# Near scans with B's product on GpSimd, the mean of D u and of near sums taken off early, and a hand-ordered tail

## The chip, the core and the metric

The kernel runs on one core of a Trainium2 chip. Five engines work side by side, each through its own list of instructions in order: TensorE (PE, matmuls into PSUM), VectorE (DVE), ScalarE (ACT), GpSimd (POOL) and SyncE (SP, which here only issues DMAs). They wait for each other through semaphores. The metric is the device time of one execution in microseconds, the median of several runs.

## What is computed

Two layers over a 64 x 64 image with 96 channels. Each layer normalises, projects to 192 inner channels, convolves 3 x 3, and runs four selective scans over the 4096 positions; their sum is normalised over the channels, gated and projected back, and added to the input. The change lies in the first layer, whose scan and end are:

```python
dt = softplus(dt @ dt_proj_w + dt_proj_b)
log_dA = einsum('bld,dn->bldn', dt, A)
dB_u = einsum('bld,bln->bldn', dt, B_mat) * u[..., None]
decay = exp(cumsum(log_dA, axis=1))
h = decay * cumsum(dB_u / (decay + 1e-12), axis=1)
y = einsum('bldn,bln->bld', h, C_mat) + u * D_skip
...
y = y1 + y2 + back(y3) + back(y4)          # rows, rows backwards, columns, columns backwards
y = _layernorm(y, ln_g, ln_b)              # over the 192 channels
y = y * silu(z)
return y @ out_proj_w
```

`decay` falls below 1e-12 after a short stretch, so that far from a scan's start `h` is almost nothing. The kernel uses this: it computes the scans of the first layer only near their starts, finds out whether that covers them, and only otherwise runs the far scans.

## The kernel before

The inner channels and positions are folded into three blocks T of 128 partitions: `u[T]` (the convolved input) and `y[T]` (the sums) are 128 x 2048. A chunk c is 512 of the 2048 columns; there are four, worked from 3 down to 0.

Work of the first layer in this order: `head` (norm, projection, convolution, gate), `near_scans` (lines 277 to 612), the branch (`tc.If`, line 1729) with `far_scans` in it, `tail` (lines 1471 to 1546). Then the second layer's head, its 384 scan steps of 128 x 1024, and its end. In the input timed the branch is not taken: the far scans do not run.

**Near part.** For each block T the first 192 steps of the four directions are laid side by side (768 columns). Buffers in order: `nu` (u gathered by TensorE), `nus` (its copy), `npj` and `nxd` (the projections to B, C and dt), `npd` (dt), then softplus in `nw`, `nln`, `nt`, `nv`; `ndt`, `ndu = dt * u` and `nS` (the running sum of dt) are each copied to the other half of the partitions by SP's DMAs (`across`). Of the 16 states, taken in pairs m, the first pair is kept for 192 steps, the second for 64, the other six for 32 (`kinds`). That gives six units j: block T with 768 columns (the first pair) or with 256 + 768 (the rest), in the order 0a, 0b, 1a, 1b, 2b, 2a. For each unit:

- `operands`: `nna = exp(-A dt)` on ScalarE, with GpSimd clearing the first column of each part
- `weights_of`: `nnwt`, a tanh of S, on ScalarE
- `scan`: VectorE multiplies B by du into `nb` (PSUM), multiplies by 1 + `nnwt`, scans into `nnh`; GpSimd (VectorE in the last unit) makes `nnhc = nnh * C`
- `add`: TensorE sums the pairs into `ny` (PSUM), and after both units of a block `sum_up` adds `ny` to `y[T]` on VectorE

B comes from TensorE: a 0/1 matrix `picked` spreads each row of B over 64 partitions, into the four PSUM banks `nB`. C goes to DRAM (`nC`) and comes back spread over the partitions (`ncb`). `y` itself begins as u times D: `later`, six passes on GpSimd (`start_y`) at the beginning. `reach` and `reached` work out the flag of the branch. `look_ahead` issues the second layer's weights on SP; `ds` of the second layer is reduced on VectorE when its part of them has landed.

**Tail.** For each chunk: `centre` (mean of y over the channels by TensorE with the matrix `pos`, taken off by VectorE, then squared on ScalarE), `scale` (variance by TensorE, then rstd by Ln and Exp on ScalarE), `gated` (two operations on VectorE for each block), `project` (TensorE, then the add to the residual, the statistics for the next norm, and the store).

What sets the order: instructions issued through `pe`, `act`, `dve`, `pool` and `sp` keep the order in which they are written; those issued through `nc.vector` and so on, as in this tail, are placed by the framework's scheduler. ScalarE's function tables are loaded by the kernel (`load_exp_ln` loads the one that has Exp and Ln both) and, where a function might be called without its table, by the framework, which adds a load ahead of it.

Most instructions of the near part carry the line of the recording helper, 271, in the profile; tile names tell them apart.

Of the kernel before, what the change touches and what calls it, by code (L numbers as in the profile page):

```python
# [9 lines left out]
F32 = mybir.dt.float32  # L10
BF16 = mybir.dt.bfloat16
AF = mybir.ActivationFunctionType
ALU = mybir.AluOpType
# [31 lines left out]
def two_ss2d_layers(  # L45
# [231 lines left out]
    def near_scans(weights, later):  # L277
# [5 lines left out]
        with ExitStack() as sc:  # L283
# [5 lines left out]
            def parts(t):  # L289
# [9 lines left out]
            kinds = ((NEAR, 0, 1),) + FEWER  # L299
            top = once.tile([128, len(kinds), 3, 4], F32, name="top")  # L300
            most = once.tile([128, len(kinds) + 1, 3], F32, name="most")
            flag = once.tile([1, 1], mybir.dt.int32, name="flag")
            picked = once.tile([32, NP, 128], F32, name="picked")
            nc.gpsimd.tensor_copy(
                picked.rearrange("p m (h w) -> p m h w", h=2),
                i3[0:32, 0:NS].rearrange("p (m h) -> p m h", h=2)
                .unsqueeze(3)
                .to_broadcast([32, NP, 2, 64]),
            )
            for start in later:  # L310
                start()


            us = once.tile([128, 3, 2, 2 * NEAR], F32, name="nus")
            k = NEAR // HW
            pj = pps.tile([128, 2, 512], F32, tag="m", name="npj")[0:NC, :, 0 : 2 * NEAR]
            for T in range(3):
                ps = pps.tile(
                    [128, 4 if T == 2 else 2, 512], F32, tag="yBB"[T], name=f"nu{T}"
                )[:, 0:2]  # L320
# [18 lines left out]
                for q, copy in enumerate((act.copy, dve.tensor_copy)):  # L339
                    copy(us[:, T, q], ps[:, q, 0 : 2 * NEAR])  # L340
            for T in range(3):
                for q in range(2):
                    pe.matmul(
                        pj[:, q], xw[HALF[q], 0, T, :], us[HALF[q], T, q],
                        start=(T == 0), stop=(T == 2),
                    )
# [6 lines left out]
            C = []  # L353
            for w, m0, m1 in kinds:
                rows = dram.tile([NS, 4 * w], F32, name=f"nC{w}")
                sp.dma_start(
                    out=rows.rearrange("n (d w) -> n d w", w=w),
                    in_=parts(xd[NC - NS : NC])[:, :, 0:w],
                )
                C.append(rows)  # L360


# [62 lines left out]
            def reach():  # L425
# [10 lines left out]
                pe.transpose(Bf[0:1, at : at + 128], most[:, len(kinds), 0:1], ident)  # L436

            def reached():
                ps = Bf[0:1, at : at + 128]
                dve.reduce_max(most[0:1, len(kinds), 1:2], ps, axis=AX.X)  # L440
                dve.tensor_scalar(flag, most[0:1, len(kinds), 1:2], GONE, None, ALU.is_le)


            Bp = pps.tile([128, 4, 512], F32, tag="B", name="nB")
            Bf = Bp.rearrange("p a b -> p (a b)")
            B, cb, at = [], [], 0
            for n, m0, m1 in kinds:
                B.append([])
                t = once.tile([128, m1 - m0, 4 * n], F32, name=f"ncb{n}")
                for m in range(m0, m1):  # L450
                    dst = Bf[:, at : at + 4 * n]
                    if n == NEAR:
                        for s in (slice(0, 512), slice(512, WN)):
                            pe.matmul(
                                dst[:, s], picked[:, m, :], xd[0:32, s], start=True, stop=True
                            )
                    else:
                        pe.matmul(
                            dst.rearrange("p (d w) -> p d w", w=n), picked[:, m, :],
                            parts(xd[0:32])[:, :, 0:n], start=True, stop=True,  # L460
                        )
                    at += 4 * n
                for h, half in enumerate(HALF):
                    rows = C[len(cb)][2 * m0 + h : 2 * m1 : 2]
                    sp.dma_start(out=t[half], in_=rows.unsqueeze(0).to_broadcast(t[half].shape))
                B[-1] = Bf[:, at - 4 * n * (m1 - m0) : at]
                cb.append(t.rearrange("p n w -> p (n w)"))
# [4 lines left out]
            live = {}  # L472
# [40 lines left out]
            def scan(j):  # L513
                T, ks = units[j]
                a, wt, h, hc = live[j]

                b = pps.tile([128, 2, 512], F32, tag="m", name=f"nb{j}")
                b = b.rearrange("p a w -> p (a w)")
                o = 0
                for i in ks:  # L520
                    n, m0, m1 = kinds[i]
                    k = m1 - m0
                    dve.tensor_mul(
# [5 lines left out]
                b = b[:, 0:o]  # L529
                dve.scalar_tensor_tensor(b, wt, 1.0, b, ALU.add, ALU.mult)  # L530
# [50 lines left out]

            steps_of(0)
            steps_of(1)
            sums_of(0)
            steps_of(2)
# [6 lines left out]
            look_ahead()  # L592
            for j in range(len(units)):
# [4 lines left out]
                scan(j)  # L598
                if j == 1:
                    reach()  # L600
                if j == 2:
                    reached()
                if j == 4:
                    sum_up(1)
                add(j)
                if j == 3:
                    sum_up(0)
            sum_up(2)
            return nc.values_load(
# [860 lines left out]

    def tail(l, w, xT):
# [3 lines left out]
        with ExitStack() as sc:  # L1475
# [3 lines left out]
            sz = {}  # L1479
            for c in order:  # L1480
                for T in range(3):
# [3 lines left out]
                    nc.sync.dma_start(out=t, in_=szd[l][T, :, HT * c : HT * (c + 1)])  # L1485
                cut = slice(TC * c, TC * (c + 1))
                nc.sync.dma_start(out=xT[:, cut], in_=xs[:, cut])
            live = {}

            def centre(c):  # L1490
                cut = slice(HT * c, HT * (c + 1))
                pm = fps.tile([128, HT], F32, tag="m", name=f"m_{l}_{c}")
                for T in range(3):
                    nc.tensor.matmul(pm, pos, y[T][:, cut], start=(T == 0), stop=(T == 2))
                for T in range(3):
                    nc.vector.tensor_sub(y[T][:, cut], y[T][:, cut], pm)
                    sq = live[c, T] = fin.tile([128, HT], F32, tag=f"sq{T}", name=f"sq{l}_{c}_{T}")
                    nc.scalar.activation(sq, y[T][:, cut], AF.Square)

            def scale(c):  # L1500
                cut = slice(HT * c, HT * (c + 1))
                pv = fps.tile([128, HT], F32, tag="v", name=f"v_{l}_{c}", bufs=1)
                for T in range(3):
                    nc.tensor.matmul(pv, pos, live[c, T], start=(T == 0), stop=(T == 2))
                rstd = live[c] = fin.tile([128, HT], F32, tag="rstd", name=f"rstd{l}_{c}")
                if c == order[0]:
                    load_exp_ln()
                nc.scalar.activation(rstd, pv, AF.Ln, bias=eps5)
                nc.scalar.activation(rstd, rstd, AF.Exp, scale=-0.5)

            def gated(c):
                cut = slice(HT * c, HT * (c + 1))
                rstd = live.pop(c)
                for T in range(3):
                    q = live[c, T] = fin.tile([128, HT], F32, tag=f"g{T}", name=f"g{l}_{c}_{T}")
                    gain, bias = v[:, T, V_G : V_G + 1], v[:, T, V_B : V_B + 1]
# [304 lines left out]
```

## Time and profile before

| | us |
|---|---|
| median of 3 runs | 1474.97 |
| lowest, highest | 1471.23, 1476.99 |
| the profiled execution | 1471.02 |
| its span, first to last instruction | 1469.2 |
| near part, from the first nu matmul | 74.0 to 146.7 |
| the branch, nothing runs | 146.7 to 149.4 |
| tail of the first layer, to the last statistics | 149.4 to 192.8 |

A row of the timeline gives start, duration, engine, line, operation, the tile written and those read, and in brackets how long the engine stood idle before it and what ended the wait. A row of groups gives the count, busy microseconds, mean nanoseconds of one, and the idle time before them. A row of stages gives each engine's busy time in a stretch, TensorE's granted clock and the DMA engines' busy share. SPq is SP's queue of DMA issues. A span is the slowest core's; here there is only one.

### The profile page before, as it was taken

The numbers are of one execution on the slowest core, as the hardware profiler recorded it, in microseconds if no ns is written. First come the engines' busy times: TensorE is split into PE (matmuls) and PEld (weight loads), VectorE is DVE, ScalarE is ACT, GpSimd is POOL, SyncE is SP. The second block draws the span as 40 slices with busy tenths as digits, with TensorE's granted clock in tenths as the row PEclk, the third lists the DMA queues.
The fourth block names the chain that finished last, engine by engine and source line by source line (L and its number), as shares of the span: only waits on it lengthen the run. The fifth ranks groups of instructions, "written<-read, shape, count | busy, mean of one in ns | idle before, by whom it ended". The sixth has DMA issues, their size and how long they took to land.

```text
span 1469.2 us, 17235 instructions
## 1 busy us (share of the span) xinstructions
PE 1205.7 (82%) x5011; PEld 469.7 (32%) x5011; DVE 1338.4 (91%) x925; ACT 1216.5 (83%) x2506; POOL 1211.8 (82%) x667
## 2 busy tenths in 40 slices
PE   5845869788888797978888888887888888887887
PEld 2233313333333332333333333333333333322333
DVE  5967677789999999999999999999999999999996
ACT  5764437699998989999999999899898989897874
POOL 2753039688989898989898989898989898989894
PEclk7965979599999999999999999999999899999999
DMA  3231522526262626262626262626262726262533
GB/s 108 76 100 24 149 52 90 131 58 145 58 145 58 145 59 144 60 144 60 144 59 144 60 143 60 144 59 143 60 148 61 151 61 144 69 147 68 136 107 108
DMA packets 85556, 147.70 MB, mean 101 GB/s; under 512 B 33436, under 2 KB 36700, under 8 KB 85356
## 3 DMA queue, kind: packets, MB, share of 16 engines
q1 hardware_dynamic: 83772, 143.96, 41.3%
q0 software_dynamic: 576, 1.57, 0.5%
q10 hardware_dynamic: 1104, 0.98, 0.2%
q8 instruction: 41, 0.67, 0.2%
q14 instruction: 63, 0.52, 0.1%
HBM read 80.85 MB, written 12.13 MB: 63 GB/s over the span
## 4 chain that ended last, share of the span: by engine, by line
DVE 28%; issue 22%; PE 11%; POOL 11%; ACT 9%; DMA 6%; SPq 2%; DVEq 0%; POOLq 0%; ACTq 0%
DVE h L751 18%; DVE b L751 8%; POOL hc L751 7%; DMA cb<-C 4%; ACT a L751 3%; PE ys L751 3%; ACT bT L751 2%; SPq L751 2%; PE pj L751 2%; POOL sp L751 2%; PE b L751 1%; POOL ln L751 1%; DMA xT<-xs 1%; PE cp L271 1%; DMA dt<-sp 1%
## 5 line engine op out<-in xcount | busy, mean ns | idle before, releaser
L751 POOL TENSOR_TENSOR hc<-h,cb 128x1024 f32<-128x1024 f32 x384 | 901.9, 2368 | 93.6 <-DMA cb<-C 35.6
L751 DVE TENSOR_TENSOR_SCAN h<-a,carry,b 128x1024 f32<-128x1024 f32 x288 | 665.0, 2338 | 23.4 <-POOL hc L751 1.7
L751 ACT ACTIVATE a<-dt,am 128x1024 f32<-128x1024 f32 x384 | 438.0, 1141 | 57.3 <-DVE h L751 53.8
L751 PE MATMUL ys<-hc,fold 128*64 128x512 f32 x1536 | 429.3, 638 | 0.1
L751 ACT ACTIVATE bT<-duT,BT 128x192 f32<-128x192 f32 x1012 | 386.6, 445 | 2.9 <-PE b L751 0.9
L751 PE MATMUL b<-ident,bT 128*128 128x128 f32 x1536 | 224.3, 289 | 31.0 <-DVE h L751 19.3
L751 DVE TENSOR_TENSOR b<-b,du 128x1024 f32<-128x1024 f32 x192 | 232.0, 1208 | 6.8 <-PE b L751 6.8
L751 DVE TENSOR_TENSOR_SCAN h<-a,b 128x1024 f32<-128x1024 f32 x96 | 216.4, 2278 | 13.7 <-PE b L751 5.3
L751 PEld LDWEIGHTS b<-ident,bT 128*128 128x128 f32 x1536 | 177.0, 146 | 156.3 <-DVE h L751 89.5
L751 PE MATMUL b<-B,selh 96*128 96x512 bf16 x384 | 116.6, 385 | 126.3 <-DVE h L751 125.8
L751 PEld LDWEIGHTS ys<-hc,fold 128*64 128x64 f32 x1536 | 77.7, 138 | 138.5 <-issue 98.2
L751 PEld LDWEIGHTS <-selh 96*128 96x128 bf16 x384 | 25.6, 97 | 254.3 <-DVE h L751 203.8
L271 POOL TENSOR_TENSOR tap<-tap,tap 128x512 f32<-128x512 f32 x48 | 60.9, 1273 | 44.6 <-ACT tap L271 42.2
L751 PE MATMUL pj<-u,xw 64*124 64x512 f32 x192 | 94.1, 635 | 2.2 <-DVE w L751 1.2
L271 DVE SCALAR_TENSOR_TENSOR acc<-pad,v,acc 128x1052 f32<-128x1052 f32 (+1 forms) x64 | 75.2, 1181 | 2.1
L751 ACT CAST B<-pj 96x512 bf16<-96x512 f32 (+2 forms) x96 | 54.9, 575 | 4.5 <-PE pj L751 4.5
L751 PE MATMUL ys<-y,ident 128*128 128x512 f32 (+1 forms) x120 | 57.7, 581 | 0.0
L751 POOL TENSOR_TENSOR sp<-sp,ln 128x512 f32<-128x512 f32 x45 | 57.5, 1279 | 0.2
L751 POOL TENSOR_TENSOR ln<-ln,w 128x512 f32<-128x512 f32 x45 | 57.6, 1280 | 0.0
L751 POOL TENSOR_TENSOR su<-sp,u 128x512 f32<-128x512 f32 x45 | 57.3, 1274 | 0.0
L751 PE MATMUL pd<-xd,dwb 29*64 29x512 f32 x192 | 54.7, 639 | 0.0
L751 PEld LDWEIGHTS pj<-u,xw 64*124 64x124 f32 x192 | 33.8, 191 | 60.1 <-issue 45.7
(188 smaller groups left out, 1185.9 us busy)
## 6 DMA issues: line engine op xcount, KB each, us to landing
cb<-C SPq DMA_DIRECT2D x256, 256.0 KB
dt<-sp SPq DMA_DIRECT2D x192, 128.0 KB
du<-su SPq DMA_DIRECT2D x180, 128.0 KB
szd<-sz SPq DMA_DIRECT2D x24, 256.0 KB
szt<-szd SPq DMA_DIRECT2D x24, 256.0 KB
xT<-xs SPq DMA_DIRECT2D x8, 384.0 KB
xs<-xT SPq DMA_DIRECT2D x1, 1536.0 KB
xs<-xT SPq DMA_DIRECT2D x8, 192.0 KB
```

What stands on the lines that cost most here:

```text
L271: return lambda *args, **more: tc.keep_in_program_order(op(*args, **more))
L751: return lambda *args, **more: tc.keep_in_program_order(op(*args, **more))
```

## The change

In `near_scans`:

- B goes to DRAM and comes back spread over the partitions as C does (`stored`, `fetched`): rows of 64 steps are cut from those of 192, so that there are two stores instead of three for each of the two. The fetch of C's shorter rows is issued after block 1's transfers. `picked` and the matmuls of `nB` go.
- B's product with du is made by GpSimd (`inputs`), into SBUF tiles `nb`, the first two ahead of the units and then two units ahead; VectorE's product with the weights reads it and writes PSUM (`nbw`).
- `later` is no longer run. Instead TensorE forms the mean over the channels of D u (`mean`, with `average` = `pos` scaled by D, made by ScalarE), and VectorE writes y = D u - mean (`centre`), for chunks 3 and 2 before the units and 1 and 0 after units 0 and 1.
- The near sums change the mean of near positions again: `near_mean` forms the mean of y there (it is D u's centred value plus the near sums), `near_centre` takes it off, after the last sum. A matmul with `zeros` opens the accumulation.
- PSUM: `nu` uses three buffers instead of two; `npj` and the flag's transpose have one of their own.

In the tail: no mean and no centring; the order on each engine is written out; block 2 is gated by GpSimd with ScalarE in between (`pool_gated`), blocks 0 and 1 by VectorE; `load_exp_ln` stands at the beginning. Where the far scans run, `centre_all` takes the mean off after them.

```diff
+            for T in range(3):
+                act.mul(average[:, T], pos, ds[:, T : T + 1])
+            def mean(c):
...
+                for T in range(3):
+                    pe.matmul(
+                        ps, average[:, T], u[T][:, HT * c : HT * (c + 1)],
+                        start=(T == 0), stop=(T == 2),
+                    )
+            def centre(c):
...
+                    dve.scalar_tensor_tensor(
+                        y[T][:, s], u[T][:, s], ds[:, T : T + 1], ps, ALU.mult, ALU.subtract
+                    )
...
+            rows = stored("B", 0)
+            B = [fetched("B", rows, i) for i in range(len(kinds))]
+            rows = stored("C", NC - NS)
+            cb = [fetched("C", rows, 0)]
...
-            def scan(j):
+            def inputs(j):
...
-                    dve.tensor_mul(
+                    pool.tensor_mul(
                         b[:, o : o + 4 * n * k].rearrange("p (n d w) -> p n d w", n=k, w=n),
                         B[i].rearrange("p (n d w) -> p n d w", n=k, w=n),
                         four(du, T)[:, :, 0:n].unsqueeze(1).to_broadcast([128, k, 4, n]),
                     )
...
-                dve.scalar_tensor_tensor(b, wt, 1.0, b, ALU.add, ALU.mult)
+                dve.scalar_tensor_tensor(b, wt, 1.0, live.pop(("b", j))[:, 0:w], ALU.add, ALU.mult)
...
             steps_of(0)
+            inputs(0)
+            inputs(1)
             steps_of(1)
+            cb += [fetched("C", rows, i) for i in range(1, len(kinds))]
             sums_of(0)
+            mean(3)
+            mean(2)
...
             look_ahead()
+            for c in (3, 2):
+                centre(c)
+            for c in (1, 0):
+                mean(c)
             for j in range(len(units)):
...
                 scan(j)
+                if j < 2:
+                    centre(1 - j)
+                if j + 2 < len(units):
+                    inputs(j + 2)
...
                 if j == 4:
                     sum_up(1)
+                    near_mean(0)
+                    near_mean(1)
                 add(j)
                 if j == 3:
                     sum_up(0)
             sum_up(2)
+            near_mean(2)
+            for T in range(3):
+                near_centre(T)
```

The tail after the change, its order and the two kinds of gating:

```python
def pool_gated(c, T):
    q, gain, bias = result(c, T)
    pool.tensor_mul(q, y[T][:, at(c)], live["r", c])
    act.activation(q, q, AF.Identity, bias=bias, scale=gain)
    pool.tensor_mul(q, q, sz[c, T])
...
load_exp_ln()
squares(3)
variance(3)
squares(2)
root(3)
for c in order:
    if c:
        variance(c - 1)
    pool_gated(c, 2)
    for T in (0, 1):
        gated(c, T)
    if c > 1:
        squares(c - 2)
    if c:
        root(c - 1)
    project(c)
    if c < NCH - 1:
        add(c + 1)
add(0)
```

`squares`, `variance`, `root`, `gated`, `project` and `add` do what the steps of the same kind did before.

## The prediction

> **What bounds the kernel now.** I read the span in slices first (layer 1's scans, from 250 us on, keep VectorE at nine tenths and the diff does not touch them), then cut the part that it does touch into stages, then read each engine's timeline there. The stages:
>
> ```profile
> core 0: us, PE busy (x) PEld busy (x) DVE busy (x) ACT busy (x) POOL busy (x), PEclk, DMA share, GB/s
> 103.00:146.70 43.70, 19.36 (x57) 13.28 (x57) 32.88 (x47) 20.75 (x50) 11.79 (x16) 0.56 0.25 45
> 146.70:149.40 2.70, 0.00 (x0) 0.00 (x0) 0.00 (x0) 0.00 (x0) 0.00 (x0) 0.80 0.04 12
> 163.00:192.80 29.80, 23.61 (x72) 7.93 (x70) 29.45 (x46) 10.01 (x21) 1.52 (x13) 0.94 0.40 96
> ```
>
> The near scans are a chain through VectorE with holes (32.9 of 43.7 us busy); the branch costs 2.70 us in which nothing runs, and starts when VectorE's last near sum ends; the tail from 163 on is VectorE without a hole (29.45 of 29.80). The timeline, with what each row waited for:
>
> ```profile
> 76.42 16.95 POOL L271 TENSOR_SCALAR y<-u,ds 128x1024 f32<-128x1024 f32 x6
> 84.85 2.91 DVE L247 TENSOR_SCALAR am<-am 128x24 f32<-128x24 f32 x1
> 87.80 2.79 DVE L248 TENSOR_SCALAR am<-am 128x24 f32<-128x24 f32 x1
> 91.42 0.49 ACT L271 ACTIVATE nw<-npd 128x384 f32<-128x384 f32 x1 [2.69 <-DVE nv L271]
> 102.65 1.20 SPq L271 DMA_DIRECT2D nS<-nS  x2
> 105.52 1.03 ACT L271 ACTIVATE nnwt<-nS,lneps,am 128x768 f32<-128x768 f32 x1 [2.38 <-DMA nS<-nS]
> 144.74 1.95 DVE L271 TENSOR_TENSOR y<-ny,y 64x192 f32<-64x192 f32 x6 [3.02 <-PE ny L271]
> 160.30 1.28 ACT L85 ACT_TABLE_LOAD   x1
> 161.60 0.69 ACT L1508 ACTIVATE rstd<-v,eps 128x512 f32<-128x512 f32 x1
> 162.32 0.63 ACT L1509 ACTIVATE rstd<-rstd 128x512 f32<-128x512 f32 x1
> ```
>
> Two operations on 24 elements take 2.9 us each because GpSimd's six passes of 2.83 us run beside them; ScalarE then waits 2.69 us for VectorE. The first scan's weights wait for the transfer of S, the tenth of a queue of half-tile transfers. One table load serves the tail's Ln and Exp. Groups of the tail, by shape:
>
> ```profile
> L1520 DVE SCALAR_TENSOR_TENSOR g<-g,v,szt 128x512 f32<-128x512 f32 x12 | 8.6, 746 | 0.1
> L1517 DVE SCALAR_TENSOR_TENSOR g<-y,v,rstd 128x512 f32<-128x512 f32 x12 | 8.6, 745 | 3.5 <-ACT rstd L1509 3.4
> L1496 DVE TENSOR_TENSOR y<-y,m 128x512 f32<-128x512 f32 x12 | 7.7, 679 | 5.5 <-PE m L1494 5.5
> L1498 ACT ACTIVATE sq<-y 128x512 f32<-128x512 f32 x12 | 7.2, 627 | 34.8 <-DVE y L1496 34.7 <-DMA szt<-szd 0.2
> ```
>
> **What the Trainium skill says.** "ScalarE: Activation LUTs", What ACT_TABLE_LOAD costs: a load takes about 1283 ns and a drain about 1380 ns more. The trace agrees on the load (1.28) and shows no drain (the next operation starts 1.30 after); I use 1.30. "SBUF — State Buffer", Who interferes with whom: VectorE in a two-port mode, or with two SBUF inputs while GpSimd reads SBUF, blocks against GpSimd for whole instructions. The two am rows agree with the first half; against the second, VectorE's wl operations on two SBUF inputs took 0.69 us beside GpSimd's TENSOR_SCALAR at 256.7 and without it at 261.0. No row shows them beside a GpSimd TENSOR_TENSOR. "TensorE: Matmul & The Clock Gate", Part 1: TensorE is at half clock until it has been busy for some microseconds. Agrees: 0.50 from 88 to 132, and 0.61 and then 1.00 after the tail's matmuls begin at 149.5.
>
> **The change part by part.** *Start of the near part.* The third nu tile no longer shares a buffer with the second: the 1.16 us that PE waits at 79.37 goes. GpSimd's 16.95 us of y go too, so the am operations take some 0.2 us each: the softplus of block 1 starts at 87.7 instead of 91.4, and all that follows on ScalarE is 3.7 us earlier. The three `average` products (0.30 each, the diag row) fit in the 0.93 us in which ScalarE waits before nus.
>
> *The SP queue takes it back.* In the built program of the changed kernel 31 transfers stand ahead of the first pair of S, from the ab load at 83.6 on (before: 84.7), at 0.64 each: that pair is issued at 103.4 (before: 102.65). Ahead of it lie 384 KB of C before dt and 512 KB after du, at about 200 GB/s (the rate from 90 to 94), and eight half tiles of 96 KB at 0.65 us each: S lands 1.3 us later than before (0.8 if only the issue counts, 2.8 if C moves at the 152 GB/s of the half tiles). So the weights of unit 0 start at 106.8, those of unit 1 end at 113.8 (before: 112.6).
>
> *The units.* VectorE loses the nine products with B (6 x 0.96 + 3 x 0.43 = 7.1 us) and gains twelve centre operations of about 0.72 (8.6 us). Of these six stand before unit 0's weights are there (cover: the wait for S; without it they cost 4.3 us), three beside unit 1's tanh, three after scan 1 with no cover: 2.2 us. Unit by unit: scan 0 ends at 110.7, scan 1 at 117.5, scan 2 at 123.2 (before 121.1). GpSimd makes hc (1.81 or 2.54) and then the product two units on (the same), so product 3 is ready at 122.7, against 123.65 when VectorE asks. Scan 3 ends at 127.3 (126.4), sum 0 at 129.3. Now the missing product counts: scan 4 ends at 132.9 (133.6). TensorE's 6.3 us of ny, which wait for sum 0, end at 135.7, sum 1 at 137.7 (136.8). Ahead of the last two adds TensorE now has the zeros and two near means; at full clock, having been busy for 6 us, 0.8 + 1.3 + 1.3 us, the last behind sum 1. hc of the last unit is ready at 141.6 (141.7), the last sum ends at 146.2 (146.7).
>
> *After the last sum, uncovered:* the third near mean, eight records of 192 or 96 columns (1.3 us at full, 2.2 at half clock, taken as 1.9), and twelve small subtractions at the 0.33 of the near sums, 3.9 us, with two hand-overs 0.2: 6.0 us. The branch, and with it the tail, starts at 152.2 + 2.7 instead of 149.4: **+5.5 us**.
>
> *The tail.* Gone are twelve subtractions (7.7 us of VectorE) and four mean products. But the built program moves the tail's one load of the common Ln and Exp table ahead of the branch, where only one of the two ways is sure to pass it, and puts a load of its own before the squares, before every Ln and before every Exp: nine in the tail and two in the next head where there was one. From the tail's start: load 1.30, six squares 3.65, load, Ln, load, Exp (1.3 + 0.7 + 1.3 + 0.65): first rstd at 9.05 (before 13.6). From one rstd to the next, all in ScalarE's order: GpSimd's product 1.27 with 0.2 of hand-over, the affine 0.60, three squares 1.82, loads, Ln and Exp 3.95: 7.84 us; twice so, and once without squares, 6.02: last rstd at 30.75. VectorE needs only 5.8 us a chunk and waits. Then four g operations, 3.1, the third chunk's add and statistics 2.6, the last one's 2.6: end at 39.0, where it was 192.8 - 149.4 = 43.4: **-4.4 us**. The next head's Exp meets one more load: **+1.3 us**. Loads of szt and xT (17 us of DMA) land before they are asked for, and SP's weights end about 44 us in, before the borders at 52.
>
> *Two SBUF inputs.* The weight product in the near units has its second operand in SBUF now (it was in PSUM), and the g operations, which had both there, now run beside GpSimd's TENSOR_TENSOR. Nothing (the wl rows) to whole blocking: then units 1 to 4 wait 0.5, 0.6, 1.5 and 0.6 us, of which 2.6 stay at the last sum, and the tail's last chunk 2.6, together 5.2. I take 1.2, six weight products at the 0.19 by which one nw operation at 91.3 was longer than its fellows.
>
> Sum: 5.5 - 4.4 + 1.3 + 1.2 = +3.6 us on the profiled execution's own 1471.0 us (span 1469.2 and 1.8 around it). The median of the runs, 1474.97, lies 4.0 above it, so 1478.5. This kernel's runs spread by 0.4%, so that half a per cent, 7.4 us, is about what can be told from no change.
>
> **The rivals.** *Whole blocking between VectorE and GpSimd:* 5.2 in place of 1.2, +7.6: 1482.5. For it: the page and the am rows; against: the wl rows. *TensorE stays at half clock* after sum 0 (it decides from add 4 on): zeros 1.5, two means 2.2 each, add 4 at 4.1 and add 5 at 3.0 put the last sum at 150.6 instead of 146.2, +4.4 and 0.3 in the last mean; with the 1.2 +8.3: 1483.3, slower. For it: the clock of 0.50 through most of the stage; against: 0.71 from 132 to 140 after less work. *The loads stay hidden*, VectorE bounds the tail: rstd from 5.2 on, end at 30.2, -13.2 and no 1.3; without blocking 5.5 - 13.2 = -7.7: 1467.3. For it: 10 us of ScalarE against 30 of VectorE in the tail before; against: a load stands between each Ln and its Exp, where nothing can hide it.
>
> **How the numbers follow.** Forecast 0.56, blocking 0.18, half clock 0.14, hidden loads 0.12. The first lies within half a per cent nearly whole, 0.07 of it above; the blocking case is half above; most of the half-clock case is above: slower 0.27, faster 0.10, same 0.63. Range 1468 to 1487: from the hidden loads' time to that of half clock with S 1.5 us later and 2 us for the spread of a median.
>
> **What would show it.** Right: eleven loads of 1.28 on ScalarE in the tail and the next head, rstd 7.8 us apart, VectorE's am rows near 0.2, S landing near 106.8, and some 6 us between the last sum and the branch. Wrong: g or nbw operations of more than a microsecond (blocking), near means of 2 us (half clock), or VectorE without holes in the tail (loads hidden).

## The result and the profile after

The changed kernel takes 1484.1 us (median of 15 runs, 1478.09 to 1493.08); the kernel before, run beside it, 1471.23 (1465.64 to 1480.17). The ratio is 1.0088, with a 95% interval from 1.0067 to 1.0109: slower by 12.9 us, where 3.6 were forecast. A second set of six runs gave 1.0104 (1.0076 to 1.0131). The profiled execution took 1493.08 us, 9 above the median, at a mean granted TensorE clock of 0.922 (0.932 in the median run); a second profile of the same kernel has a span of 1483.6 at 0.927.

To compare profiles whose heads begin at slightly different times, I count from the start of the last eight z matmuls of the first head, which the change leaves alone. All entries are us from the timelines; the branch is counted up to VectorE's first instruction behind it (the memset of dwb), the tail from there to the aggregation of its statistics, the next head to the first operation on wl in layer 2, and the rest to the end of the span.

| profile | z to last near sum | mean of near tokens, and branch | tail | next head | rest of layer 2 | clock |
|---|---|---|---|---|---|---|
| before | 74.55 | 2.95 | 43.24 | 63.78 | 1212.5 | 0.930 |
| before, again | 72.31 | 2.96 | 43.42 | 63.91 | 1214.1 | 0.940 |
| after | 78.13 | 6.76 | 43.79 | 66.21 | 1222.8 | 0.922 |
| after, again | 78.11 | 7.00 | 43.39 | 66.16 | 1216.2 | 0.927 |

To the first wl operation the two kernels differ by 11.2 us (means of two), and every stage has a part in it: 4.7, 3.9, 0.3 and 2.3. The tail, which was to pay for the rest, gained nothing. Stages of the profile after: the near units up to the last sum, the mean of near tokens with the branch, and the tail behind its first rstd:

```profile
core 0: us, PE busy (x) PEld busy (x) DVE busy (x) ACT busy (x) POOL busy (x), PEclk, DMA share, GB/s
107.50:151.57 44.07, 23.28 (x85) 14.46 (x83) 35.44 (x44) 22.00 (x50) 22.06 (x22) 0.70 0.22 44
151.57:158.14 6.57, 1.16 (x8) 0.72 (x8) 3.08 (x12) 0.00 (x0) 0.00 (x0) 0.73 0.02 6
171.80:201.60 29.80, 20.99 (x56) 6.38 (x56) 24.77 (x29) 20.03 (x29) 10.05 (x20) 0.83 0.42 104
```

VectorE, which gave nine products away in the near units (7.1 us), is busier there than before (35.4 against 32.9 us). Six of the twelve centre operations stand in this stretch (4.1 us), the six products with the weights take 11.0 us instead of 6.6, and the three operations on top, which work out the flag, 1.4 instead of 0.3. In the tail ScalarE's busy time has doubled (20.0 us, where it was 10.0). First two weight products of the kernel before, then rows of the near part after:

```profile
112.66 1.23 DVE L271 SCALAR_TENSOR_TENSOR nb<-nnwt,nb 128x1024 f32<-128x1024 f32 x1
118.27 0.96 DVE L271 SCALAR_TENSOR_TENSOR nb<-nnwt,nb 128x768 f32<-128x768 f32 x1
```

```profile
85.53 0.17 DVE L247 TENSOR_SCALAR am<-am 128x24 f32<-128x24 f32 x1
85.73 0.18 DVE L248 TENSOR_SCALAR am<-am 128x24 f32<-128x24 f32 x1
...
103.22 2.61 SPq L271 DMA_DIRECT2D nCb<-nC  x4
105.94 1.21 SPq L271 DMA_DIRECT2D nS<-nS  x2
...
109.96 1.03 ACT L271 ACTIVATE nnwt<-nS,lneps,am 128x768 f32<-128x768 f32 x1 [6.25 <-DMA nS<-nS]
...
124.90 2.42 DVE L271 SCALAR_TENSOR_TENSOR nbw<-nnwt,nb 128x768 f32<-128x768 f32 x1
...
129.47 2.75 DVE L271 SCALAR_TENSOR_TENSOR nbw<-nnwt,nb 128x1024 f32<-128x1024 f32 x1
...
131.09 3.47 POOL L271 TENSOR_TENSOR nb<-nBb,ndu 128x256 f32<-128x256 f32 x2
...
136.52 1.28 ACT L85 ACT_TABLE_LOAD   x1
...
149.60 1.97 DVE L271 TENSOR_TENSOR y<-ny,y 64x192 f32<-64x192 f32 x6 [1.66 <-PE ny L271]
...
152.82 3.18 DVE L271 TENSOR_TENSOR y<-y,nmn 64x174 f32<-64x174 f32 x12 [1.25 <-PE nmn L271]
```

The am operations fell from 2.9 to 0.2 us. But S is issued later and lands later. The weight product took 0.96 us for 768 columns and 1.23 for 1024 when one of its operands lay in PSUM; now it takes 1.8 to 2.75 in four of the six units (two of them shown), each time beside a product of GpSimd's. I call this blocking. GpSimd suffers too: 3.47 us for a pair of products that took 2.51 for the unit before. The load at 136.52 is the one of Exp and Ln that the tail's code asks for: the built program runs it ahead of the branch. The tail's groups, where the kernel before had a single table load:

```profile
L271 ACT ACT_TABLE_LOAD x10 | 12.8, 1283 | 20.5 <-DVEq L1811 20.3
L271 DVE SCALAR_TENSOR_TENSOR g<-y,v,rstd 128x512 f32<-128x512 f32 x8 | 10.2, 1276 | 12.4 <-ACT rstd L271 12.4
L271 DVE SCALAR_TENSOR_TENSOR g<-g,v,szt 128x512 f32<-128x512 f32 x8 | 8.8, 1106 | 0.3
```

The g operations average 1.28 and 1.11 us where they took 0.75. Sixteen of them cost VectorE 19.0 us, and the 24 of before cost 17.2: the third that went to GpSimd bought nothing. VectorE's g operations for the third chunk and for the beginning of the last one, the last rstd, two projections, and the last wait:

```profile
183.93 1.86 DVE L271 SCALAR_TENSOR_TENSOR g<-y,v,rstd 128x512 f32<-128x512 f32 x1
185.83 0.75 DVE L271 SCALAR_TENSOR_TENSOR g<-g,v,szt 128x512 f32<-128x512 f32 x1
186.50 1.75 DVE L271 SCALAR_TENSOR_TENSOR g<-y,v,rstd 128x512 f32<-128x512 f32 x1
188.29 0.75 DVE L271 SCALAR_TENSOR_TENSOR g<-g,v,szt 128x512 f32<-128x512 f32 x1
...
189.09 1.96 PE L271 MATMUL o<-g,op 64*96 64x512 f32 x8 [1.35 <-DVE g L271]
189.41 0.63 ACT L271 ACTIVATE rstd<-rstd 128x512 f32<-128x512 f32 x1
191.60 0.73 DVE L271 SCALAR_TENSOR_TENSOR g<-y,v,rstd 128x512 f32<-128x512 f32 x1
192.36 1.81 DVE L271 SCALAR_TENSOR_TENSOR g<-g,v,szt 128x512 f32<-128x512 f32 x1
...
195.68 3.57 PE L271 MATMUL o<-g,op 64*96 64x512 f32 x8 [0.35 <-DVE g L271]
...
199.30 0.69 DVE L271 TENSOR_TENSOR xT<-o,xT 96x512 f32<-96x512 f32 x1 [1.04 <-PE o L271]
```

None of VectorE's rows of the third chunk has a wait in brackets. VectorE, slowed, no longer keeps up even with a ScalarE that is slowed by its loads: the last rstd is ready at 190.04 us, and VectorE takes it up at 191.60.

### The profile page after: what moved, and what is told of

Same layout as the page of the kernel before. It is cut to its first block, busy times and chain, and to the rows that moved or that the text cites. A ratio compares the mean times of both kernels' runs of the same rounds, so it can differ in the third digit from the quotient of the medians.

```text
span 1491.1 us, 17293 instructions
## 1 busy us (share of the span) xinstructions
PE 1225.7 (82%) x5019; PEld 471.8 (32%) x5019; DVE 1338.8 (90%) x920; ACT 1234.6 (83%) x2524; POOL 1220.4 (82%) x678
## 4 chain that ended last, share of the span: by engine, by line
DVE 23%; issue 19%; PE 14%; ACT 13%; POOL 8%; DMA 8%; SPq 5%; DVEq 0%; POOLq 0%; ACTq 0%
DVE h L805 15%; DVE b L805 6%; POOL hc L805 5%; DMA cb<-C 4%; ACT a L805 4%; PE pj L805 4%; SPq L805 3%; ACT bT L805 3%; PE ys L805 3%; PE b L805 2%; DMA dt<-sp 2%; DMA szt<-szd 1%; POOL sp L805 1%; PE cp L271 1%; POOL ln L805 1%
## 5 line engine op out<-in xcount | busy, mean ns | idle before, releaser
L805 PE MATMUL ys<-hc,fold 128*64 128x512 f32 x1536 | 434.0, 645 | 0.6 <-POOL hc L805 0.5
L805 DVE TENSOR_TENSOR b<-b,du 128x1024 f32<-128x1024 f32 x192 | 232.1, 1209 | 11.4 <-PE b L805 11.4
L805 PE MATMUL pj<-u,xw 64*124 64x512 f32 x192 | 101.4, 677 | 1.7 <-DVE w L805 1.2
L805 PE MATMUL ys<-y,ident 128*128 128x512 f32 (+1 forms) x120 | 61.0, 610 | 0.0
```

Source lines behind the costliest of these rows:

```text
L805: return lambda *args, **more: tc.keep_in_program_order(op(*args, **more))
```

## The experiments

All are edits of the changed kernel unless said otherwise. Beside each time stands its ratio to the kernel before, run with it. Theory A is the table loads, B the blocking between VectorE and GpSimd, C the mean of near tokens, D the place of S on SP's queue; what each expects stands in the text put down before the run. Times after "the z matmuls" count from their start, as in the table above.

### One table load for the tail

```diff
-            load_exp_ln()
             squares(3)
             variance(3)
             squares(2)
+            load_exp_ln()
             root(3)
```

> The changed kernel with one edit: the tail's load of the common Ln and Exp table stands behind the squares of the first two chunks instead of at the start, so that one load serves the tail, as before the change (11 loads fewer). Theory A, the loads are what the tail lost: first rstd 6.4 us after the tail's start instead of 9.8, the next ones less than 6 us apart, tail 33 us instead of 43.9, the next head 1.3 us shorter: 12 us less than the changed kernel's 1484.1, about 1472. Theory B, VectorE's g operations held up by GpSimd's products (8 of 16 took 1.63 to 1.86 us instead of 0.75) bound the tail as soon as the loads are gone: rstd early, but a chunk still takes VectorE 7.5 us or more, tail 37 to 39 us: about 1477.

Measured: 1474.48 us, ratio 1.0021 (1.0008 to 1.0034), between the two theories. The tail takes 37.24 us instead of 43.4 to 43.8, which is theory B's number: the loads cost 6.3 us there, and behind them stands VectorE. The next head takes 65.07 instead of 66.2; what the load costs there is set out below. VectorE's two groups of g operations, in this kernel's tail:

```profile
L271 DVE SCALAR_TENSOR_TENSOR g<-y,v,rstd 128x512 f32<-128x512 f32 x8 | 9.6, 1199 | 7.5 <-ACT rstd L271 7.5
L271 DVE SCALAR_TENSOR_TENSOR g<-g,v,szt 128x512 f32<-128x512 f32 x8 | 8.7, 1085 | 0.3
```

The idle time before them has fallen from 12.4 to 7.5 us, nearly all of it the wait for the first rstd; the operations are nearly as long as without this edit.

### One operand of the g operations in PSUM

This stands on top of the edit above. The variance has one PSUM buffer instead of two besides.

```diff
+                rp = live["rp", c] = fps.tile([128, HT], F32, tag="rp", name=f"rp{l}_{c}")
+                act.activation(rp, r, AF.Exp, scale=-0.5)
                 act.activation(r, r, AF.Exp, scale=-0.5)
...
+                p = fps.tile([128, HT], F32, tag="gp", name=f"gp{l}_{c}_{T}", bufs=1)
                 dve.scalar_tensor_tensor(
-                    q, y[T][:, at(c)], gain, live["r", c], ALU.mult, ALU.mult
+                    p, y[T][:, at(c)], gain, live["rp", c], ALU.mult, ALU.mult
                 )
-                dve.scalar_tensor_tensor(q, q, bias, sz[c, T], ALU.add, ALU.mult)
+                dve.scalar_tensor_tensor(q, p, bias, sz[c, T], ALU.add, ALU.mult)
```

> As e1_table, and in the tail rstd is made twice by ScalarE, once in PSUM for VectorE and once in SBUF for GpSimd, and the g operations' intermediate lies in PSUM: each of VectorE's two g operations has one operand in SBUF. Theory B (two SBUF operands beside GpSimd's products is what blocks): all 16 g operations at 0.75 us or less, GpSimd's at 1.27, tail 31 to 32 us, 5 to 7 us less than e1_table, about 1470. Theory A (only the loads counted): no difference from e1_table except 0.65 us of ScalarE a chunk, 0 to 2 us more.

Measured: 1469.78 us, 0.9996 (0.9969 to 1.0023); tail 33.41 us. The same two groups:

```profile
L271 DVE SCALAR_TENSOR_TENSOR g<-gp,v,szt 128x512 f32<-128x512 f32 x8 | 6.0, 750 | 0.4
L271 DVE SCALAR_TENSOR_TENSOR gp<-y,v,rp 128x512 f32<-128x512 f32 x8 | 6.0, 750 | 9.3 <-ACT rp L271 9.2
```

All sixteen are back at 750 ns, and the tail is 3.8 us shorter, though ScalarE makes rstd twice. What changed for VectorE is where one input of each g operation, and the first one's result, lies: theory B holds in the tail, with less than was expected of it (5 to 7 us).

### The near weights in PSUM

The buffer of the flag's transpose moves from tag j to tag B besides.

```diff
+                wt = pps.tile([128, 2, 512], F32, tag="mj"[j % 2], name=f"nwt{j}")
+                wt = live["wt", j] = wt.rearrange("p a w -> p (a w)")
...
-                b = pps.tile([128, 2, 512], F32, tag="m", name=f"nbw{j}")
-                b = b.rearrange("p a w -> p (a w)")[:, 0:w]
-                dve.scalar_tensor_tensor(b, wt, 1.0, live.pop(("b", j))[:, 0:w], ALU.add, ALU.mult)
+                b = live.pop(("wt", j))[:, 0:w]
+                dve.scalar_tensor_tensor(b, b, 1.0, live.pop(("b", j))[:, 0:w], ALU.add, ALU.mult)
```

> The changed kernel with one edit in the near part alone: the weights nnwt (tanh of S) are written to PSUM, in two buffers by turns, and VectorE's product with GpSimd's nb is made in place there, so that it has one operand in SBUF. Theory B (blocking is what the near part lost): the product takes 0.97 us in every unit instead of 2.02, 2.42, 2.75 and 1.82 in units 1 to 4, GpSimd's nb at 2.5 and 1.8, and the last near sum is 3 to 5 us earlier: about 1480. Theory C (the near part lost by S landing 2.3 us later and by the mean and the subtractions after the last sum, 4.4 us): VectorE then waits for GpSimd's products or for hc instead, the last sum less than 1.5 us earlier: about 1483.

Measured: 1487.04 us (7 runs, median clock 0.928), 1.0098 (1.0064 to 1.0131). The time shows no gain; its interval is too wide for an effect of 2 us, and I go by the trace. The products of units 2 and 3 in VectorE's timeline:

```profile
123.65 0.95 DVE L271 SCALAR_TENSOR_TENSOR nwt<-nwt,nb 128x768 f32<-128x768 f32 x1
...
126.75 1.23 DVE L271 SCALAR_TENSOR_TENSOR nwt<-nwt,nb 128x1024 f32<-128x1024 f32 x1
```

The blocking of these products is gone, 4.4 us by the sum over units 1 to 4 (9.0 and 4.6). The last sum comes 75.76 us after the z matmuls instead of 78.12, so 2.4 us of it were on the path; the rest turned into waits for the weights. After the last sum the near mean and the branch take some 0.6 us more, as TensorE's eight matmuls took 1.74 us instead of 1.16. This lies between the two theories: B in kind, half of it in size.

### All three

The three edits above in one kernel.

> The edits of e1_table, e2_tail_psum and e3_near_psum together. If loads (12 to 13 us) and blocking (tail with the loads gone 5 us, near 4 us) are the whole of what went wrong: near part 2.5 us longer than before the change, tail 12 us shorter, about 1466, that is 5 us below the kernel before (1471.2). If the near part's loss is S and the mean after the last sum: 1469 to 1470. If the layer 2 that this change leaves alone is slower for its own reason by some 3 us (the part of the 12.9 us that the stages do not give): 3 us more than each of these.

Measured: 1469.81 us, 0.9995 (0.9976 to 1.0015): no faster than the tail's two edits alone, within the interval. By the trace the last sum is at 75.78 and the tail takes 33.80: the edits keep what they gave singly. To the first wl operation it is 3.6 us ahead of the first profile of before and 1.6 ahead of the second. A slower layer 2 does not show: 1213.4 us at a clock of 0.932.

### The kernel before, again

> The kernel before, once more, for a second profile of it. The stages that the change leaves alone vary from execution to execution: layer 2 from its first VectorE operation on wl to the end took 1212.5 us in the first profile of before (granted clock 0.930), 1222.8 in that of the changed kernel (0.922) and 1209.6 to 1217.5 in the four experiments (0.930 to 0.938). If the clock alone sets it (5.5 us for each 0.01 in the lists of runs), this profile lies at 1212.5 less 5.5 us for each 0.01 above 0.930, within 3 us. If the changed kernels have a slower layer 2 of their own, it lies 2 to 4 us below them at the same clock. The near part from the last z matmuls on ends its last sum 74.5 us later and the tail takes 43.4 us, within 0.3 us.

Measured: 1471.54 us in the profiled run. The tail repeats; the near part does not. Its last sum comes 2.2 us sooner than in the first profile, all of it in VectorE's waits for TensorE's sums of the second and third block (0.37 and 1.66 us here, 1.30 and 3.02 there). TensorE's last six matmuls of these sums took 1.56 us here, at a granted clock of 0.92 from 140 to 144 us, and 2.93 there, at 0.51 from 141 to 145. The profile that the forecast was built on had the slower near part of the two. Layer 2 missed the expected value: 1214.1 us at the higher clock, where 1207 was expected, so the mean clock of a whole run is a poor measure of that stage. Against 1209.6 to 1220.4 in the edited kernels there is no clear sign that the change slows it.

### Without the mean of near tokens

```diff
-                    near_mean(0)
-                    near_mean(1)
                 add(j)
...
-            near_mean(2)
-            for T in range(3):
-                near_centre(T)
```

> The changed kernel without the mean of near tokens: it leaves out the forming of that mean (the matmul with zeros and the three near_mean) and the twelve subtractions of near_centre. Theory C1 (the mean costs only what stands after the last sum): the last sum where it is in the changed kernel, and the branch 4.4 us sooner after it, about 1479.7. Theory C2 (TensorE's zeros and its first two near means, written ahead of the last two adds, hold those up too): the last sum 1 to 2 us sooner besides, about 1478.5. If TensorE's clock is lower in the tail for want of this work, 0.5 us is given back there.

Measured: 1482.37 us, 1.0053 (1.003 to 1.0075). The last sum is at 77.95 us, where it was 78.12, and dwb comes 2.82 us behind it instead of 6.76 to 7.00. The row behind the branch:

```profile
153.66 0.70 DVE L196 MEMSET dwb<- 32x768 f32 x1 [2.82 <-DVEq L1806]
```

So the mean costs 4.1 us, nearly all behind the last sum: theory C1. The zeros and the first two means hold the last sum up by 0.2 us at most.

### C's shorter rows behind S

```diff
-            cb += [fetched("C", rows, i) for i in range(1, len(kinds))]
             sums_of(0)
...
             weights_of(1)
+            cb += [fetched("C", rows, i) for i in range(1, len(kinds))]
             look_ahead()
```

> The changed kernel with one edit: the fetches of C's shorter rows (four transfers, 2.6 us of SP's queue) stand behind the three S transfers instead of ahead of the first. Theory D (S bounds the start of the units): S issued near 103.3 instead of 105.9, the first weights at 107.5 instead of 110.0, and the last sum 2.3 us sooner, as VectorE has hardly a hole between: about 1481.8. Rival (S waits for its producer or lands with the bytes already under way, or GpSimd's products come next): the last sum less than 1 us sooner, 1483 to 1484.

Measured: 1484.17 us (6 runs), 1.0083 (1.0051 to 1.0116): the time alone is inconclusive. The trace shows the difference:

```profile
102.87 1.20 SPq L271 DMA_DIRECT2D nS<-nS  x2
...
106.74 2.48 SPq L271 DMA_DIRECT2D nS<-nS  x4
109.27 2.61 SPq L271 DMA_DIRECT2D nCb<-nC  x4
```

The first weights start 32.88 us after the z matmuls instead of 36.52, and the last sum is at 74.69 instead of 78.12: 3.4 us, more than theory D expected. 2.4 of the 3.6 us at the weights are SP's queue, the remaining 1.2 the transfer itself: from the issue of S to the weights it takes 2.9 us instead of 4.0.

### What kind of GpSimd work blocks

```diff
-                pool.tensor_mul(q, y[T][:, at(c)], live["r", c])
+                pool.tensor_scalar_mul(q, y[T][:, at(c)], gain)
                 act.activation(q, q, AF.Identity, bias=bias, scale=gain)
-                pool.tensor_mul(q, q, sz[c, T])
+                pool.tensor_scalar_mul(q, q, gain)
```

> The changed kernel with GpSimd's two TENSOR_TENSOR a chunk in the tail replaced by TENSOR_SCALAR on the same tiles; it leaves out the products of block 2 with rstd and with the gate. Theory B1 (GpSimd's second SBUF operand is what blocks VectorE's two-operand instructions, as the wl rows beside a TENSOR_SCALAR suggested): all 16 g operations at 0.75 us, and GpSimd's own at their undisturbed length. Theory B2 (any GpSimd work that reads SBUF blocks them): 6 or more of the 16 still take 1.4 us or longer.

This was one profiled run. Measured: neither theory. Rows of GpSimd and VectorE in one chunk of this kernel's tail:

```profile
173.46 1.56 POOL L271 TENSOR_SCALAR g<-g,v 128x512 f32<-128x512 f32 x1 [2.89 <-ACT g L271]
173.48 1.21 DVE L271 SCALAR_TENSOR_TENSOR g<-g,v,szt 128x512 f32<-128x512 f32 x1
...
175.39 1.06 DVE L271 SCALAR_TENSOR_TENSOR g<-g,v,szt 128x512 f32<-128x512 f32 x1
```

Beside a TENSOR_SCALAR seven of the sixteen are longer, by 0.2 to 0.5 us, not by 0.9 to 1.1. (The tail's 36.94 us can't be set against the others: its affine, the step on ScalarE between GpSimd's two, no longer waits for rstd.) That the wl operations of before showed no lengthening at all beside GpSimd's TENSOR_SCALAR is not explained by this.

### B's product back on VectorE

The calls of `inputs` ahead of the units and two units ahead go.

```diff
-                    pool.tensor_mul(
+                    dve.tensor_mul(
...
+                inputs(j)
                 scan(j)
```

> The changed kernel with the product of B and du back on VectorE, just ahead of each unit's scan; all else as changed. Theory P (GpSimd's product costs VectorE in blocking about what it saves it): 6.1 us of products in units 1 to 5 come back, 4.6 us of blocked weight products and 1.1 of top go; the last sum within 1.5 us of the changed kernel's 78.1 us after the last z matmuls began, time within 2 us of it. Theory Q (the move is worth its 6 us, blocking is small beside holes that are there anyway): the last sum 3 to 5 us later, about 1488.

Measured: 1489.42 us, 1.011 (1.0087 to 1.0132). The changed kernel, run beside it, had 1.0104 (6 runs each), so the times don't tell the two apart. By the trace the last sum comes at 80.32 us, 2.2 later: between the two theories. GpSimd's product is worth some 2 us in this kernel, not the 7 that it takes off VectorE. Two things limit what this says of the kernel before: VectorE's product reads both its operands from SBUF here, where B once lay in PSUM, and it still meets GpSimd's other product, hc. Unit 3 shows it (2.83 us, and 1.63 in unit 1, which meets less of hc):

```profile
114.84 1.63 DVE L271 TENSOR_TENSOR nb<-nBb,ndu 128x256 f32<-128x256 f32 x2
...
127.28 2.83 DVE L271 TENSOR_TENSOR nb<-nBb,ndu 128x256 f32<-128x256 f32 x2
```

### The changed kernel, again

> The changed kernel once more, on the same chip as these. The record of its first profile had a low granted clock in layer 2 (0.922). If layer 2 differs by the clock alone, the part from the first wl operation on takes 1212 to 1218 us here instead of 1222.8; the near part (78.1 us from the last z matmuls to the last sum), the tail (43.9) and the next head to the first wl operation (66.2) repeat within 1 us, and the ratio lies at 1.008, within 0.002.

Measured: 1486.4 us, 1.0104 (1.0076 to 1.0131). The stages repeat within 0.4 us, and layer 2 takes 1216.2 us: the 1222.8 of the first profile does not repeat.

### Everything that helped, together

The edits of "All three", C behind S, and `npj` taken ahead of the nu tiles:

```diff
+            pj = pps.tile([128, 2, 512], F32, tag="j", name="npj")[0:NC, :, 0 : 2 * NEAR]
             for T in range(3):
                 ps = pps.tile([128, 2, 512], F32, tag="ymB"[T], name=f"nu{T}")
...
-            pj = pps.tile([128, 2, 512], F32, tag="j", name="npj")[0:NC, :, 0 : 2 * NEAR]
```

> The edits of e4_all and e6_c_later together, and npj taken ahead of the nu tiles, so that the first nu tile no longer lies in the PSUM banks of the last z tile (nu waited 0.75 us there in all changed kernels). If the losses found so far add up: nu starts with no wait (0.8 us), S is there 3.5 us sooner, the last sum 3 to 4 us sooner than in e4_all, tail 33.5 us as there: 1466 against 1472 to 1475 for before, ratio 0.996. Rival: GpSimd's products, which wait for the du transfer, or TensorE's sums bound the near part once S is early, and the last sum comes less than 2 us sooner: ratio 0.998.

Measured: 1467.35 us (22 runs), ratio 0.9958 (0.9940 to 0.9976): faster than both kernels. nu starts without its wait, 1.87 us after the z matmuls instead of 2.68, and the weights at 31.79. But the last sum, at 75.05, is only 0.7 us earlier than in "All three", as the rival had it: the gains of the near part do not add up. To the first wl operation this kernel is 4.3 us ahead of the kernel before (mean of its two profiles): its tail is 9.8 us shorter, its near part 1.6 longer, and the mean with the branch 3.9 longer. It is 1.8 us ahead of "All three", so that most of the step in the ratio, from 0.9995 to 0.9958, is not in these stages; the two intervals meet at 0.9976. What took the rest of the near part's gain, in VectorE's timeline:

```profile
101.93 2.45 DVE L271 TENSOR_TENSOR_SCAN nsums<-steady,nv 128x384 f32<-128x384 f32 x1
104.31 3.35 DVE L271 SCALAR_TENSOR_TENSOR y<-u,ds,nm 128x512 f32<-128x512 f32 x5
...
116.00 2.06 DVE L271 SCALAR_TENSOR_TENSOR y<-u,ds,nm 128x512 f32<-128x512 f32 x3 [5.62 <-PE nm L271]
```

The last running sum now stands beside GpSimd's first product and takes 2.45 us instead of 0.96. The centring behind it is late; TensorE's next means, which need its buffer, start 34.4 us after the z matmuls instead of 32.1 in "All three" and take 8.25 us instead of 6.91; and VectorE waits 5.62 us for them where it waited for S before. The hole was moved, not closed.

### ScalarE's order in the tail

"Everything together" with the affine of block 2, and GpSimd's product after it, behind the next chunk's squares and rstd:

```diff
-                pool_gated(c, 2)
+                scaled = pool_gated(c, 2)
                 for T in (0, 1):
                     gated(c, T)
                 if c > 1:
                     squares(c - 2)
                 if c:
                     root(c - 1)
+                affine(c, 2, *scaled)
```

> As e8_best, and in the tail ScalarE makes the squares and rstd of the next chunk before the affine of block 2, which waits 1.4 us for GpSimd. VectorE waits 2.5 us for the second chunk's rstd in the tail of e2_tail_psum and e4_all: if ScalarE's order is what holds it, that wait shrinks to under 1 us and the tail takes 32 us instead of 33.5. Rival: the projection of the chunk before, later by the 3 us of the squares and rstd, holds VectorE's add instead: no gain or 1 us lost.

Measured: 1472.87 us, 0.9996 (0.9978 to 1.0013), 5.5 above "everything together"; tail 38.81 us. VectorE's wait for the second rstd did shrink, to 0.45. The rival had named the late projection, but not what it holds up. ScalarE's next two rstd, and TensorE ahead of the second of them:

```profile
173.06 0.69 ACT L271 ACTIVATE rstd<-v,eps 128x512 f32<-128x512 f32 x1 [3.75 <-PE v L271]
...
177.14 1.10 PE L271 MATMUL o<-g,op 64*96 64x512 f32 x4 [2.23 <-POOL g L271]
178.17 4.54 PE L271 MATMUL v<-sq,pos 128*128 128x512 f32 x6
182.75 0.69 ACT L271 ACTIVATE rstd<-v,eps 128x512 f32<-128x512 f32 x1 [7.00 <-PE v L271]
```

The projection (o) stands ahead of the next variance (v) in TensorE's order. It waits for GpSimd's late g, the variance waits behind it, and rstd waits for the variance.

## Why the forecast was too low, by its own steps

The stages give 11.2 us where the steps summed to 3.6. Of the 7.6 us between, the tail has 4.7, the near part with its mean 1.9 and the next head 1.0. That 1484.1 us still lies inside the forecast's range of 1468 to 1487 is in part luck: the range was built on a median of 1474.97 for the kernel before, which ran at 1471.23 beside the changed one. The same 12.9 us on 1474.97 would have been 1487.9. With half a per cent as the line, as the forecast drew it, the kernel is slower, to which the forecast gave 0.27.

*The am operations, the nu buffers.* Right: 0.2 us each, and the 1.16 us in PE's nu matmuls are gone. What was not seen is that the first nu tile now waits 0.75 us for ScalarE's last work on z; the softplus of block 1 is therefore 3.2 us earlier and not 3.7. Taking npj first removed the wait, so the order in which buffers are taken decides it.

*SP's queue and S.* Right in mechanism, short in size. Forecast +1.3 us at unit 0's weights; measured 36.52 after the z matmuls against 33.38 in both profiles of before, +3.1. The issue is 2.0 us later (forecast 0.75), of which 0.8 is the later start of nu; the landing takes 1.2 longer (forecast about 0.55).

*The units.* Forecast: last sum 0.5 us earlier, with 1.2 to come on top for two SBUF inputs. Measured: 3.6 later than in the profile used, and 5.8 later than in the second, whose sums were 2.2 us quicker. Taken alone, the near weights' edit gives back 2.4 and C's place 3.4; together, and with npj first, they give 3.1.

*After the last sum.* Forecast 6.0 us more, measured 3.9. The third mean, at a granted clock of 1.00, took 1.16 us instead of 1.9, and the subtractions 3.18 instead of 3.9; the branch behind them took 2.33 instead of 2.95, and why was not tested. Leaving the mean out gives 4.1 back. This error and that of the units have opposite signs, and that the near part as a whole is off by only 1.9 us is luck.

*The tail.* This is the step that failed. The loads, their number and their 1.28 us, were forecast rightly. The first rstd came at 9.8 us instead of 9.05 (the terms listed give 8.9, and ScalarE waits 1.36 for the first variance besides), the rest 8.25, 7.7 and 6.1 apart where 7.84, 7.84 and 6.02 were forecast. But "VectorE needs only 5.8 us a chunk and waits" was wrong: with two of its four g operations blocked it needs 7.7 (5.0 for g and 2.65 for add and statistics). It is therefore 1.6 us late for the last rstd, then loses 1.06 to a blocked operation, and then 1.04 to a projection for which the granted clock was 0.54 (3.57 us for eight records that took 1.96 a chunk earlier at 1.00). Forecast from the last rstd to the end 8.3 us, measured 12.0. So -4.4 became +0.3. This split is read from the trace: no run takes the blocking away while the loads are there.

*Two SBUF inputs.* The term taken at 1.2 us was mis-sized, and it had nothing for the tail. The Trainium skill, "SBUF — State Buffer", Who interferes with whom, had it: a VectorE instruction with two SBUF inputs contends with a GpSimd instruction that reads SBUF. I discounted it for the wl rows, and those stand beside another operation of GpSimd, TENSOR_SCALAR, where the sentence does not hold as it stands: 0.69 us with it and without it. Beside GpSimd's TENSOR_TENSOR it does: 0.6 to 1.5 us more on a weight product, 0.9 to 1.1 on a g operation. The rival "whole blocking" put 5.2 us on it and 1482.5 in all; on the path it is 2.4 in the near part by the experiment, and 3.8 in the tail once the loads no longer hide part of it.

*The next head.* Forecast +1.3 for one more load, measured +2.3. The load is as forecast: without VectorE's wait for z at xd, the head takes 62.1 to 62.3 us in the seven profiles with all the loads and 60.8 to 61.0 in the seven without. The other 1.0 is that wait (3.9 us instead of 2.9 to 3.0), which in the experiments is at times there and at times not; its cause stays open.

*TensorE at half clock* as a rival fell: the near means took 1.16 us, and leaving them out moved the last sum by 0.2. *Hidden loads* fell as well: removing them gives 6.3 us in the tail.

The stages give 11.2 us, the median 12.9. In layer 2 the twelve profiles of the changed and the edited kernels take 1209.6 to 1222.8 us and the two of before 1212.5 and 1214.1. That is no steady difference, but two profiles are too few to exclude one of 2 or 3 us. So the 1.7 us between stay open; they lie within what medians of such runs differ by (106 runs of before spread from 1466.83 to 1487.93).

## What to carry to other kernels

Before moving work from VectorE to GpSimd, count the operands that VectorE's instructions beside it read from SBUF. With two, beside GpSimd's TENSOR_TENSOR, 4.4 of the 7.1 us moved here came back as longer weight products, and GpSimd's own grew too; putting one operand in PSUM brought the old lengths back. A table load written at the start of a stage behind a branch need not stay there: here the built program set it ahead of the branch (at 136.5 us, where the branch ended at 158) and then loaded again before the squares, every Ln and every Exp. Written where it is used, behind the first squares, one load served; count the loads in the profile. When new transfers enter a shared queue, look at what they push back: here B's took C's place, and four small fetches of C came to stand ahead of S, which by itself cost 3.4 us.

## What the runs showed of the hardware that I had not expected

- The blocking depends on GpSimd's operation: VectorE's g operation of 0.75 us took 1.63 to 1.86 beside a TENSOR_TENSOR and 0.98 to 1.21 beside a TENSOR_SCALAR on tiles of the same size (one profile).
- It holds for a scan as well: a running sum of 384 elements took 2.45 us beside GpSimd's product and 0.96 without it.
- In the 106 runs of the kernel before, the time is about 5 us shorter for each 0.01 that the mean granted TensorE clock is higher, and rather more than half of the variance between runs goes with it. Set at one clock (0.935) by such a line, the changed kernel's runs lie in the mean 11.4 us above the kernel before and those of "everything together" 5.0 below it, close to the 11.2 above and 4.3 below of the stages.
